# Streaming layer 3's factors in more and smaller pieces, and making layer 2's and 3's helper rows later

## Chip, cores and metric

The kernel runs on one core of a Trainium2 chip. The metric is the device time of one execution in microseconds (us); lower is better. The time of the kernel before is 2317.83 us, the median of three runs.

## What is computed

Four graph layers on 128 graphs of 64 nodes with 512 features, in float32. `x` is [128, 64, 512] and `adj` [128, 64, 64]. Every layer takes `h = relu(layernorm(x))` and adds its result to `x`. Cut to what matters:

```python
# layer 0: hypergraph convolution 512 -> 1024, relu, layernorm, convolution 1024 -> 512
H = (adj != 0); m = Be * (H^T (h @ W1)); ...
# layer 1: attention from a sum of two scores
s = (h @ w) @ a;  A = exp(leaky(8 * tanh((s_i + s_j) / 8))) * adj, normalised;  out = A @ h @ w
# layer 2: attention from queries and keys
weight = adj * exp((h Wq^T + bq) (h Wk^T + bk)^T), normalised;  out = weight @ (h Wv^T + bv)
# layer 3: diffusion over K = 3 steps
e = leaky_relu(sj + si + ab);  transition = A * exp(e), normalised      # sj, si = (h @ Wv + bv) @ aw halves
H = sum_k Xk @ Wk[k] + bk[k],  Xk = transition^k @ h;  out = relu(H)
```

## The kernel before

**Tiles and stages.** The 8192 rows (nodes) are worked in 16 groups (`NG`) of 512 rows, four tiles of 128 rows each. The first half of the kernel runs layers 0 and 1 for all groups and stores the result in DRAM (`xmid`); the second half loads it again and runs layers 2 and 3 for all groups. Large products use a scheme of seven block products in place of eight (`strassen` for layers 0 and 1, the matmul at line 691; `chained` for layer 2, line 930; `product` for layer 3, line 1124). A float32 matmul shows as two passes in the trace.

**Layer 3's products.** For each group, `layer3` forms seven products with the weights `Wk3`. Their weight side, the factors, doesn't fit on chip for all seven. During the first half `setup_w3` makes them once and stores them in DRAM: `fac[f][n]`, with 4 blocks in `n = 0` and 3 blocks in `n = 1` (`BLOCKS`), each block 3 x 128 x 128. In the second half, `product` streams them back for every group: one load for `n = 0` (768 KB), one for `n = 1` (576 KB), at line 1116, into a buffer `wf` of up to four blocks; three such places exist. A block is then three matmuls (six passes). In the last group (`g == NG - 1`) two more buffers, `sh` and `hT`, which no later layer needs, take a part of the pieces. So a group has 14 such loads, the kernel 224.

**The helper rows.** `setup_bq` makes the vector `gb_c` from `Wk` and `bq` (layer 2): four loads of 256 KB, four multiply-adds on VectorE (lines 492 and 494), a small matmul. `setup_l3` makes the two rows `c3_b` and the constant `kap` (layer 3): twelve loads of 256 KB, ten dots on VectorE (`dot`, line 392), two spreads over the partitions (`spread`, lines 458 to 461). Both use four temporary places `tmp`, which layer 0's transposes use as well, and both are placed ahead of the loop over the groups, with priorities near group 0's.

**What sets the order.** The code doesn't emit instructions at once. Each operation goes into a `Graph` with its engine, an estimated cost, its reads and writes, and a priority: `G.prio` (period of the group, advanced by `step` as the layer proceeds) plus a shift by the name of the part (`part(name)` looks it up in `AT`). `Graph.run` then simulates five engines, `PE`, `DVE`, `ACT`, `POOL` and `SP`, and at each step takes the operation that can start first, the lowest priority first among those that can start at the same time. It also assigns the buffer places. Its result is a fixed order of instructions on every engine; on the chip each engine runs its own in that order and waits on semaphores. All DMAs go through SP's queue. Where the plan sees TensorE idle for over 1 us, `fill` puts matmuls of ones (line 1199) there.

```python
def dma(kb, fn, r, w, issue=0.34, lat=2.0):
    return G.op("SP", max(kb / 380.0, issue), fn, r, w, lat)
```

Lines named in what follows: 338 loads into `tmp`; 355 loads of `x`; 592 and 594 the graph products of layers 0 and 1; 601 to 603 a transpose by DMA (a copy, the DMA at line 602, a copy); 995 a second load of `x` in layer 2; 1067 layer 3's product with the transition; 1091 and 1104 to 1106 VectorE's block differences; 1133 the copy out of PSUM; 1163 the stores of the result.

Of the kernel before, what the change touches and what calls it, by code (L numbers as in the profile page):

```python
# [14 lines left out]
P = 128  # L15
C = 64
D = 512
DH = 1024
T = 4
KD = D // P  # L20
# [151 lines left out]
def tile_adj_preln_d4(  # L172
# [6 lines left out]
    nc = tc.nc  # L179
    NG = adj.shape[0]  # L180
    G = Graph()
# [22 lines left out]
        ([("row", [P, D], 4)], [("sh", [P, 4, 2, 2 * P], 1)]),  # L204
        ([("wa", [P, D], 1)], [("q", [P, D], 1)]),
        ([("wp", [P, 4, P], 2)], [("bv", [P, D], 1), ("bk", [P, D], 1)]),
        ([("w2m", [P, 7168], 1), ("wm", [P, 3584], 1)], [("a3", [P, 3, KD, P], 4), ("wf", [P, 4, 3, P], 3)]),
    ]
    slots, after = {}, {}
    for tag, (shape, n) in SLOTS.items():  # L210
# [8 lines left out]
    for two in TWO:  # L219
        both = work.tile([P, max(sum(size(shape) * n for _, shape, n in tags) for tags in two)], F32,  # L220
                         name="_".join(tag for tags in two for tag, _, _ in tags))
        for tags in two:
            at = 0
# [31 lines left out]
    def c_mm(n, count):  # L255
        return 2 * count * max(n * 2 / 2400 + 0.0025, 0.111)
# [6 lines left out]
    def pe(cost, fn, r, w):  # L263
        return G.op("PE", cost, fn, r, w)
# [16 lines left out]
    def dma(kb, fn, r, w, issue=0.34, lat=2.0):  # L281
        return G.op("SP", max(kb / 380.0, issue), fn, r, w, lat)

    def quad(b):
# [2 lines left out]
    FILL, LAT = 0.5, 2.3  # L287


    STRETCH, PERIOD1, PERIOD2 = (2.4057, 23.1237, 14.6194, 5.0478), 88.385, 152.83  # L290
    AT = {
        "x0": -4649.81, "apart": 515.41, "w1": 891.32, "b1": 147.15, "w2": 1055.04, "w": 146.66, "c1": 74.0, "l0":
        181.27, "c2": 131.25, "l1": 1241.14, "c": -4314.2, "g0": -2118.58, "g1": -4213.04, "g2": -574.45, "g3":
        -1827.82, "g": -443.79, "bq": -420.39, "l3": -143.58, "wg": 627.97, "wp": 228.79, "beg0": -1054.79, "beg1":
        -138.73, "end00": 1.09, "end01": -86.62, "end11": 256.44, "new2": -124.9, "new3": 81.75, "end2": -68.63,
        "end3": -133.99, "load1": -63.98, "load2": 661.26, "m": -63.44, "h0": 2.91, "p0": 25.16, "z0": -386.05,
        "q0": 47.65, "y0": -4107.25, "h1": -19.07, "p1": 5.7, "z1": -84.16, "q1": 20.96, "y1": -130.14, "s": -234.6,
        "t0": -462.0, "e0": -467.09, "t1": -348.17, "e1": -282.93, "hT": 524.3, "sh": 245.53, "lq": 730.58, "pt":
        -113.04, "v": 589.88, "pv": 1100.8, "s3": 672.72, "tt": 1008.78, "a0": 690.15, "b0": 538.95, "a1": 811.73,
        "ws": 2002.18, "load3": 441.07, "bk": 299.55,  # L300
    }

    def part(name):
        G.shift = AT[name]
# [28 lines left out]
        dma(8, lambda: nc.sync.dma_start(sb, src), [], [name])  # L333
        return sb

    def load_tmp(tag, n, shape_of, src):
        b = Buf(tag)
        dma(n * P * 4 / 1024, lambda: nc.sync.dma_start(shape_of(b.t), src), [], [b])
        return b

    def temp(src):

        return load_tmp("tmp", D, lambda t: t, src)

    xt, adjs, xmid, rows = {}, {}, {}, []

# [43 lines left out]
    def dot(in0, in1, acc, r, w):  # L390
        j = Buf("o")
        dvp(0.77, lambda: nc.vector.scalar_tensor_tensor(j.t, in0(), 1.0, in1(), op0=ALU.mult, op1=ALU.mult,
                                                         accum_out=acc()), r, [*w, j])
# [89 lines left out]
            act(0.6, lambda c=c, e=e: nc.scalar.copy(e.t, ps[c].t), [ps[c]], [e])  # L483
            dma(256, lambda c=c, e=e: nc.sync.dma_start(wg_d[c * P:(c + 1) * P, :], e.t), [e], ["wg_d"])

    def setup_bq():

        pg, bk = Buf("ps"), Buf("o")
        for o in range(KD):
            k_ = temp(Wk[o * P:(o + 1) * P, :])  # L490
            if o == 0:
                dvp(0.45, lambda k_=k_: nc.vector.tensor_scalar(bk.t, k_.t, bq_c[:, 0:1], None, op0=ALU.mult), [k_, "bq_c"], [bk])
            else:
                dvp(0.85, lambda o=o, k_=k_: nc.vector.scalar_tensor_tensor(bk.t, k_.t, bq_c[:, o:o + 1], bk.t, op0=ALU.mult, op1=ALU.add),
                    [k_, "bq_c", bk], [bk])

        def mg():
            for c in range(KD):
                nc.tensor.matmul(pg.t[:, c:c + 1], bk.t[:, c * P:(c + 1) * P], ones[:, 0:1], start=True, stop=True)
        pe(c_mm(1, KD), mg, [bk], [pg])  # L500
        dve(0.2, lambda: nc.vector.tensor_copy(gb_c, pg.t[:, :KD]), [pg], ["gb"])

    def setup_l3():
        kk = Buf("mv")
        ab_t = load_tmp("rs", 1, lambda t: t, ab.partition_broadcast(P))
        for s in range(2):
            av, cc = temp(aw[s * D:(s + 1) * D].partition_broadcast(P)), Buf("col")
            bv_t = temp(bv3.partition_broadcast(P))
            dot(lambda bv_t=bv_t: bv_t.t, lambda av=av: av.t, lambda s=s: kk.t[:, s:s + 1], [bv_t, av], [(kk, s)])
            for c in range(KD):  # L510
                wv = temp(Wv3[c * P:(c + 1) * P, :])
                dot(lambda wv=wv: wv.t, lambda av=av: av.t, lambda c=c, cc=cc: cc.t[:, c:c + 1], [wv, av], [(cc, c)])
            spread(lambda cc=cc: cc.t, lambda s=s: c3_b[:, s, :], [(cc, c) for c in range(KD)], ("c3", s))
        dve(0.15, lambda: nc.vector.tensor_add(kap, kk.t[:, 0:1], kk.t[:, 1:2]), [(kk, 0), (kk, 1)], ["kap"])
        dve(0.15, lambda: nc.vector.tensor_add(kap, kap, ab_t.t), ["kap", ab_t], ["kap"])

# [492 lines left out]
    def layer3(g):  # L1009
# [66 lines left out]


        part("b0")
        sx = Buf("sx")
        keys = lambda i, v: [(a3[2 * i + v], n) for n in range(3)]  # L1080
        block = lambda i, j: [(lambda v=v: a3[2 * i + v].t[:, :, 2 * j:2 * j + 2, :]) for v in range(2)]
# [14 lines left out]
        def product(f, F, chain, first):  # L1096
            (A, B), (ka, kb) = F
            if first:
                banks[chain] = [Buf("ps"), Buf("ps")]
            X = Buf("xi")  # L1100
            lo, hi = (lambda f_: f_()[:, :, 0, :]), (lambda f_: f_()[:, :, 1, :])
            x2, x3, x4 = ((lambda i=i: X.t[:, i]) for i in range(3))
            sub = nc.vector.tensor_sub
            dvp(0.6, lambda: sub(x2(), lo(B), lo(A)), [*ka, *kb], [(X, 0)])
            dvp(0.6, lambda: sub(x3(), hi(B), x2()), [*kb, (X, 0)], [(X, 1)])
            dvp(0.6, lambda: sub(x4(), hi(A), x2()), [*ka, (X, 0)], [(X, 2)])
            lhs = {1: (lambda: lo(A), ka), 2: (lambda: hi(A), ka), 6: (x2, [(X, 0)]), 5: (lambda: lo(B), kb),
                   7: (x3, [(X, 1)]), 3: (x4, [(X, 2)]), 4: (lambda: hi(B), kb)}
            for n in range(2):
                w_, p, q = Buf(("wf", "sh", "wf", "hT", "wf")[(2 * f + n) % 5] if g == NG - 1 else "wf"), banks[chain][n], len(BLOCKS[n])  # L1110
                wv = lambda w_=w_, q=q: w_.t[:, :q] if w_.tag == "wf" else (
                    w_.t.rearrange("p a b c -> p (a b c)") if len(w_.t.shape) == 4 else w_.t.rearrange("p a b -> p (a b)"))[:, :q * 3 * P].rearrange(
                        "p (r k c) -> p r k c", r=q, k=3)
                shift = G.shift
                part("ws")
                dma(1000 if q == 4 else 850, lambda n=n, wv=wv: nc.sync.dma_start(
                    wv(), fac[f - 1][n].rearrange("p (r k c) -> p r k c", k=3, c=P)), [("fac", f - 1, n, k, d) for k in range(3) for d in FACS[n]] + ([(tt, 1)] if g == NG - 1 else []), [w_], lat=LAT)
                G.shift = shift
                for r, b in enumerate(BLOCKS[n]):
                    at, kl = lhs[b]  # L1120

                    def mm(at=at, r=r, p=p, wv=wv, q=q):
                        for k in range(3):
                            nc.tensor.matmul(inner(p, q)[:, r, :], at()[:, k, :], wv()[:, r, k, :], start=first and r == 0 and k == 0,  # L1124
                                             stop=k == 2, skip_group_check=True)
                    pe(c_mm(P, 3), mm, [*kl, w_] if first and r == 0 else [*kl, w_, p], [p])
                    step(c_mm(P, 3))

        def snapshot(chain):
            Z = Buf("zz")  # L1130
# [60 lines left out]
    def step(us):  # L1191

        G.prio += us * stretch[0]
# [19 lines left out]
    setup_l1()  # L1213
    part("c")
    W = combine(wm, w_sb, w_x, 2, D // 2, "DVE")
    part("bq")
    setup_bq()
    part("l3")
    setup_l3()
    for g in range(NG):  # L1220
        G.prio = g * PERIOD1
        if g:
            part("load1")
            load_group(g, x_in)
        for i, layer in ((0, layer0), (1, layer1)):
            stretch[0] = STRETCH[i]
            if g == 0:
                G.prio += AT["beg0" if i == 0 else "beg1"]
            if i == 0 and g == NG - 1:
                G.prio += AT["end00"]  # L1230
            if i == 1 and g >= NG - 2:
                G.prio += AT["end01" if g == NG - 2 else "end11"]
            layer(g)
        G.prio = g * PERIOD1
        part("wp")
        if g:
            for k in range(2):
                if 2 * g - 2 + k < 21:
                    setup_w3(2 * g - 2 + k, [("z", g - 1 + k, 1 - k)], [("z", g, k)])
# [83 lines left out]
```

## Time and profile before

| | |
|---|---|
| runs (us) | 2317.83, 2319.93, 2316.39 |
| profiled execution (us) | 2321.51 |
| its span, first to last instruction (us) | 2319.7 |
| mean granted TensorE clock | 0.999 |
| busy: PE, DVE, ACT, POOL (us) | 2279.9, 1865.1, 1393.2, 1190.9 |
| DMA | 355.12 MB, mean 153 GB/s |

PE is TensorE's matmuls and PEld its weight loads, DVE VectorE, ACT ScalarE, POOL GpSimd, SP the engine whose queue issues the DMAs. A group of instructions is told as line, engine, tiles written `<-` tiles read. `fac` is the factors in DRAM; the tiles of `wf` appear as `w2m_wm_a_wf`, since several tags share one piece of memory; for the same reason the tiles of `tmp` appear as `tmp_mB_xi`, those of `hT` as `z_hT` and those of `sh` as `row_sh`. A DMA issue line gives the count, the size of each and the median time from issue to landing. The chain of waits is the work that ended last, followed back from the last instruction. In a table by stretches, each row gives start:end, length, then the busy time of PE, PEld, DVE, ACT and POOL with the number of instructions in brackets, the granted clock, the busy share of the DMA engines and GB/s.

### The profile page before, as it was taken

To read this page: it belongs to the slowest core of one execution; us is meant where nothing else is said; L and a number is where in the kernel's file an instruction comes from. 1 tells how busy PE (TensorE), PEld (TensorE's weight loads), DVE (VectorE), ACT (ScalarE), POOL (GpSimd) and SP (SyncE) were. 2 spreads that over 40 slices of the span, in tenths; PEclk is the share of its full clock that TensorE was granted. 3 is DMA by queue.
4 is the path that set the end of the run, shared out by engine and by line. 5 is a ranking of instruction groups with operands and counts; after the bars stand their busy time and mean duration, and the time that the engine had idled before them with its cause. 6 is when DMAs were issued, how large, how long until landed. Compare 5 with 4: busy or idle time off the path is not lost.

```text
span 2319.7 us, 39752 instructions
## 1 busy us (share of the span) xinstructions
PE 2279.9 (98%) x14238; PEld 1866.4 (80%) x14238; DVE 1865.1 (80%) x4004; ACT 1393.2 (60%) x1993; POOL 1190.9 (51%) x1771
## 2 busy tenths in 40 slices
PE   8999999999999999999999999999999999999998
PEld 4676677776777767777688999999999989999898
DVE  7887877887778877787867888888888878788787
ACT  4766565675655765656657566566656655656542
POOL 7445556545665465543433455545455544545443
PEclk9999999999999999999999999999999999999999
DMA  6443233443333342323436877787787877878767
GB/s 232 103 104 77 78 98 79 102 90 79 83 91 94 90 90 58 74 71 68 97 98 161 223 222 229 234 223 213 226 244 213 235 215 217 222 224 225 200 200 242
DMA packets 403478, 355.12 MB, mean 153 GB/s; under 512 B 290896, under 2 KB 321872, under 8 KB 403280
## 3 DMA queue, kind: packets, MB, share of 16 engines
q1 hardware_dynamic: 403280, 352.58, 55.5%
q8 instruction: 112, 1.84, 0.3%
q14 instruction: 86, 0.70, 0.1%
HBM read 241.05 MB, written 44.33 MB: 123 GB/s over the span
## 4 chain that ended last, share of the span: by engine, by line
PE 84%; DMA 6%; DVE 5%; ACT 3%; issue 1%; POOL 1%; SPq 0%; DVEq 0%; ACTq 0%; POOLq 0%
PE ps L691 38%; PE ps L1124 19%; PE ps L930 15%; PE ps L592 4%; PE ps L844 2%; PE ps L1067 2%; DMA w2m_wm_a_wf<-fac 1%; DMA h<-o 1%; PE ps L999 1%; PE ps L961 1%; DMA x<-xm 1%; DMA z_hT<-tmp_mB_xi 1%; ACT h L583 1%; DVE st L562 1%; DMA tmp_mB_xi<-in_Wk_dram 0%
## 5 line engine op out<-in xcount | busy, mean ns | idle before, releaser
L583 ACT ACTIVATE h<-x,nm,rs 128x512 f32<-128x512 f32 x384 | 306.2, 812 | 234.9 <-POOL nm L570 220.3
L564 POOL TENSOR_SCALAR rs<-mv 128x1 f32<-128x1 f32 x320 | 104.6, 327 | 388.4 <-DVE mv L563 371.1
L1124 PE MATMUL ps<-w2m_wm_a_wf 128*128 128x128 f32 x2256 | 295.5, 277 | 3.8 <-DMA w2m_wm_a_wf<-fac 2.2
L1124 PEld LDWEIGHTS ps<-w2m_wm_a_wf 128*128 128x128 f32 x2256 | 275.8, 192 | 11.1 <-issue 4.0
L691 PE MATMUL ps<-w2m_wm_a_wf,s_s_zz 128*128 128x256 f32 x1152 | 274.8, 380 | 1.8 <-DVE s_s_zz L683 1.8
L1124 PE MATMUL ps<-w2m_wm_a_wf,tmp_mB_xi 128*128 128x128 f32 x1968 | 260.4, 277 | 9.8 <-DMA w2m_wm_a_wf<-fac 5.2
L1124 PEld LDWEIGHTS ps<-w2m_wm_a_wf,tmp_mB_xi 128*128 128x128 f32 x1968 | 243.2, 193 | 16.6 <-ACT h L583 7.5
L691 PEld LDWEIGHTS ps<-w2m_wm_a_wf,s_s_zz 128*128 128x128 f32 x1152 | 217.7, 190 | 39.7 <-issue 9.6
L691 PE MATMUL ps<-w2m_wm_a_wf,rT_vu_tt 128*128 128x256 f32 x1024 | 237.5, 380 | 2.0 <-ACT row_sh L453 0.7
L691 PE MATMUL ps<-wa_mem,mT_sx 128*128 128x512 f32 x512 | 238.1, 593 | 1.3 <-DMA wa_mem<-in_W1T_dram 1.0
L691 PEld LDWEIGHTS ps<-w2m_wm_a_wf,rT_vu_tt 128*128 128x128 f32 x1024 | 193.6, 190 | 48.5 <-issue 18.4
L565 POOL TENSOR_TENSOR rs<-rs,mhalf 128x1 f32<-128x1 f32 x320 | 209.2, 654 | 26.5
L562 DVE BATCH_NORM_STATS2 st<-x 128x6 f32<-128x512 f32 x256 | 176.1, 688 | 33.0 <-DMA x<-xm 25.7
L570 POOL TENSOR_SCALAR nm<-mv,rs 128x1 f32<-128x1 f32 x320 | 171.4, 537 | 30.2
L691 PE MATMUL ps<-wa_mem,s_s_zz 128*128 128x512 f32 x384 | 180.3, 593 | 0.0
L691 PEld LDWEIGHTS ps<-wa_mem,mT_sx 128*128 128x128 f32 x512 | 96.0, 191 | 103.9 <-issue 97.9
L818 ACT ACTIVATE z_hT<-z_hT 128x512 f32<-128x512 f32 x128 | 79.3, 630 | 133.6 <-DVE z_hT L711 133.6
L603 ACT COPY rT_vu_tt<-z_hT 128x1024 uint16<-128x1024 uint16 x128 | 146.7, 1162 | 16.6 <-DMA z_hT<-tmp_mB_xi 16.5
L719 POOL TENSOR_TENSOR u<-u,row_sh 128x256 f32<-128x256 f32 x96 | 75.4, 794 | 157.3 <-DVE u L661 134.7
L592 PEld LDWEIGHTS ps<-bd,h 128*128 128x128 f32 x1024 | 126.6, 192 | 36.4 <-issue 27.6
L885 POOL TENSOR_TENSOR x<-x,u 128x256 f32<-128x256 f32 x96 | 88.8, 950 | 113.0 <-DVE u L663 113.0
L601 ACT COPY o<-h 128x1024 uint16<-128x1024 uint16 x128 | 133.8, 1047 | 9.3 <-DVE h L1056 6.9
(205 smaller groups left out, 4991.8 us busy)
## 6 DMA issues: line engine op xcount, KB each, us to landing
w2m_wm_a_wf<-fac SPq DMA_DIRECT2D x110, 768.0 KB, 5.0
w2m_wm_a_wf<-fac SPq DMA_DIRECT2D x109, 576.0 KB, 4.8
x<-xm SPq DMA_DIRECT2D x128, 256.0 KB, 3.5
x<-in_x_dram SPq DMA_DIRECT2D x64, 256.0 KB, 2.8
xm<-x SPq DMA_DIRECT2D x64, 256.0 KB, 2.0
out_dram<-x SPq DMA_DIRECT2D x64, 256.0 KB, 3.9
adj<-in_adj_dram SPq DMA_DIRECT2D x32, 256.0 KB, 4.6
fac<-wp_bv_bk SPq DMA_DIRECT2D x63, 128.0 KB, 2.0
```

What stands on the lines that cost most here:

```text
L562: dve(0.69, lambda i=i: nc.vector.bn_stats(st.t[:, i, :], src(i)), [r[i]], [(st, i)])
L564: small(0.28, lambda: nc.gpsimd.tensor_scalar_add(rs.t, mv.t[:, 1:2], EPS), [mv], [rs])
L565: small(0.62, lambda: nc.gpsimd.tensor_tensor(rs.t, rs.t, mhalf, ALU.pow), [rs], [rs])
L570: small(0.32, lambda: nc.gpsimd.tensor_scalar(nm.t, mv.t[:, 0:1], rs.t, -1.0, op0=ALU.mult, op1=ALU.mult), [mv, rs], [nm])
L583: act(0.82, lambda: nc.scalar.activation(h.t, xx.t, AF.Relu, bias=nm.t, scale=rs.t), [xx, nm, rs], [h])
L592: nc.tensor.matmul(quad(p)[:, c, :], h.t[:, c * P:(c + 1) * P], rhs(), start=True, stop=True)
L601: act(1.05, lambda: nc.scalar.copy(u16(planes.t).rearrange("p (q c) -> p q c", q=2), u16(src()).rearrange("p (c q) -> p q c", q=2)), ksrc, ...
L603: act(1.16, lambda: nc.scalar.copy(u16(dst()).rearrange("p c (k q) -> p c k q", q=2), u16(back()).rearrange("p (q c r) -> p c r q", q=2, c ...
L691: nc.tensor.matmul(p.t[:, :n], lhs()[:, c, :], rhs(c), start=first and c == 0, stop=c == kc - 1, skip_group_check=True)
L885: pool(0.78, lambda: nc.gpsimd.tensor_add(xx.t[:, cols], xx.t[:, cols], U.t[:, iu]), [xx, u], [xx])
L930: nc.tensor.matmul(pair(p.t)[:, o, :], a, b, start=first and o == 0 and c == 0, stop=c == 1, skip_group_check=True)
L1124: nc.tensor.matmul(inner(p, q)[:, r, :], at()[:, k, :], wv()[:, r, k, :], start=first and r == 0 and k == 0, stop=k == 2, skip_group_check ...
```

## The change

- The streamed factors have pieces of two blocks (384 KB) or one (192 KB). A product has four loads: 2 and 2 blocks of `n = 0`, 2 and 1 of `n = 1`. `wf` has six places of two blocks, in the same memory as three of four blocks. In the last group, every eighth piece goes to `sh` and every eighth to `hT`. The plan's cost of a load goes from 1000 and 850 to 495 and 290.
- `setup_bq` is called after group 2's layers are put into the graph, and `setup_l3` in two halves after those of groups 3 and 4. Their loads wait (`when`) for an operation of layer 0 of that group (the last small operation before line 831's normalisation).
- Layer 3 of the last two groups gets a further shift of priority from its part `b0` on (`late3`, `last3`).
- All values of `STRETCH`, `PERIOD1`, `PERIOD2` and `AT` are other ones.

```diff
-        ([...], [("a3", [P, 3, KD, P], 4), ("wf", [P, 4, 3, P], 3)]),
+        ([...], [("a3", [P, 3, KD, P], 4), ("wf", [P, 2, 3, P], 6)]),
...
-    STRETCH, PERIOD1, PERIOD2 = (2.4057, 23.1237, 14.6194, 5.0478), 88.385, 152.83
+    STRETCH, PERIOD1, PERIOD2 = (2.471, 24.4862, 13.5943, 6.202), 83.899, 164.599
     AT = {
-        "x0": -4649.81, "apart": 515.41, "w1": 891.32, ...
+        "x0": -62.74, "apart": -18.5, "w1": -4.8, ...
...
-    def setup_bq():
+    def setup_bq(when):
...
-            k_ = temp(Wk[o * P:(o + 1) * P, :])
+            k_ = temp(Wk[o * P:(o + 1) * P, :], when)
...
-    def setup_l3():
-        kk = Buf("mv")
-        ab_t = load_tmp("rs", 1, lambda t: t, ab.partition_broadcast(P))
-        for s in range(2):
...
+    def setup_l3(s, when):
+        if not s:
+            sums.append((Buf("mv"), load_tmp("rs", 1, lambda t: t, ab.partition_broadcast(P), when)))
+        kk, ab_t = sums[0]
+        av, cc = temp(aw[s * D:(s + 1) * D].partition_broadcast(P), when), Buf("col")
+        bv_t = temp(bv3.partition_broadcast(P), when)
...
         part("b0")
+        if g >= NG - 2:
+            G.prio += AT["late3" if g == NG - 2 else "last3"]
...
-                w_, p, q = Buf(("wf", "sh", "wf", "hT", "wf")[(2 * f + n) % 5] if g == NG - 1 else "wf"), banks[chain][n], len(BLOCKS[n])
...
-                dma(1000 if q == 4 else 850, lambda n=n, wv=wv: nc.sync.dma_start(
-                    wv(), fac[f - 1][n].rearrange("p (r k c) -> p r k c", k=3, c=P)), ..., [w_], lat=LAT)
...
-                for r, b in enumerate(BLOCKS[n]):
...
+                p, q = banks[chain][n], len(BLOCKS[n])
+                for lead in range(0, q, 2):
+                    m, at_ = min(2, q - lead), 4 * f + 2 * n + lead // 2
+                    w_ = Buf({2: "sh", 6: "hT"}.get(at_ % 8, "wf") if g == NG - 1 else "wf")
...
+                    dma(495 if m == 2 else 290, lambda n=n, wv=wv, lead=lead, m=m: nc.sync.dma_start(
+                        wv(), fac[f - 1][n][:, lead * 3 * P:(lead + m) * 3 * P].rearrange("p (r k c) -> p r k c", k=3, c=P)),
+                        ..., [w_], lat=LAT)
...
+                    for r in range(lead, lead + m):
...
-    part("bq")
-    setup_bq()
-    part("l3")
-    setup_l3()
+    sums = []
     for g in range(NG):
...
         part("wp")
+        if g in (2, 3, 4):
+            part("bq" if g == 2 else "l3")
+            when = [("z", g, 0)]
+            setup_bq(when) if g == 2 else setup_l3(g - 3, when)
+            part("wp")
```

## The prediction

> **What bounds the kernel now.** I read the page first: busy shares, then the chain, then the DMA issues.
>
> ```profile
> span 2319.7 us, 39752 instructions
> ...
> PE 2279.9 (98%) x14238; PEld 1866.4 (80%) x14238; DVE 1865.1 (80%) x4004; ACT 1393.2 (60%) x1993; POOL 1190.9 (51%) x1771
> ...
> w2m_wm_a_wf<-fac SPq DMA_DIRECT2D x110, 768.0 KB, 5.0
> w2m_wm_a_wf<-fac SPq DMA_DIRECT2D x109, 576.0 KB, 4.8
> x<-xm SPq DMA_DIRECT2D x128, 256.0 KB, 3.5
> ```
>
> TensorE is busy 98% of the span, and the change takes no matmul away. So all it can win is TensorE's idle time, 2319.7 - 2279.9 = 39.8 us, and the 138 filler passes (line 1199) that the plan puts into gaps it foresees, about 0.112 us each, 15 us. A part of this cannot be had: the first loads and the last output (about 7 us after the last matmul).
>
> Where that time lies is seen in stretches of 58 us (PE busy is the second figure, DVE the fourth):
>
> ```profile
> 0.00:58.00 58.00, 51.11 (x204) 28.57 (x205) 41.58 (x88) 26.19 (x42) 41.10 (x59) 1.00 0.67 232
> 58.00:116.00 58.00, 55.17 (x209) 36.51 (x208) 51.67 (x103) 41.91 (x58) 25.11 (x35) 1.00 0.43 103
> 116.00:174.00 58.00, 56.29 (x275) 43.89 (x274) 48.56 (x114) 36.64 (x50) 26.93 (x44) 1.00 0.42 104
> 406.00:464.00 58.00, 58.00 (x258) 42.53 (x257) 47.30 (x108) 36.12 (x51) 29.68 (x48) 1.00 0.41 101
> 1218.00:1276.00 58.00, 54.52 (x415) 48.57 (x415) 44.55 (x106) 42.68 (x61) 21.39 (x42) 1.00 0.64 162
> 1856.00:1914.00 58.00, 54.78 (x486) 50.51 (x486) 46.07 (x100) 33.65 (x49) 27.41 (x38) 1.00 0.79 215
> 2204.00:2262.00 58.00, 55.82 (x523) 52.60 (x522) 50.55 (x108) 28.33 (x43) 24.64 (x32) 1.00 0.67 202
> 2262.00:2320.00 58.00, 48.51 (x458) 46.46 (x456) 42.35 (x78) 14.67 (x24) 21.89 (x27) 0.98 0.75 240
> ```
>
> The first half in its steady run (406 to 464) has no idle TensorE at all. The losses are the start, the turn from layer 1 to layer 2 (1218 to 1276), single bad groups of the second half (1856 to 1914) and the end. The granted clock is 1.00 nearly throughout, so the clock explains nothing.
>
> What TensorE waits for comes from its waits at line 1124, layer 3's products (us, times), and then from the chain between 1840 and 1925 us (start, length, what):
>
> ```profile
>   DMA w2m_wm_a_wf<-fac: 9.8, 11
> ```
>
> ```profile
> 1848.29 5.18 PE ps L930 x24
> ...
> 1884.84 4.88 DMA w2m_wm_a_wf<-fac
> ...
> 1892.97 4.89 PE ps L1124 x42
> ...
> 1903.38 6.13 DMA w2m_wm_a_wf<-fac
> ...
> 1919.66 5.18 PE ps L930 x24
> ```
>
> The block "L930 x24" comes once a group; in the chain of waits it starts at 1372.24, 1439.70 and so on to 2125.14 us. Eleven groups take 752.9 us, 68.4 each, and the quickest takes 67.46. So the steady second half loses 11 x 0.99 = 10.9 us. The group above takes 71.37, 3.9 too many, and two late factor loads stand in it. Two more long groups (69.46 and 68.33) hold such loads too; the three lose 6.8 us between them.
>
> **The pieces.** A piece is now 4 or 3 blocks in one of three places. Forty-two passes, one product of 7 blocks, take 4.69 us when nothing holds them. When a piece is used up, its place is refilled while TensorE works through the two other pieces, 7 blocks, 4.69 us. The refill takes 5.0 or 4.8 us from issue to landing. It is late by some tenths whenever no other work of TensorE comes between; that agrees with few, short waits: 11, 9.8 us. After the change there are six places of 2 blocks (one piece in four has 1). Five other pieces hold 8.75 blocks on average, 8.75 / 7 x 4.69 = 5.9 us. No row shows a load of 384 KB; it lies between 3.5 us (256 KB) and 4.8 us (576 KB), by their line 4.0. I take 4.0, and the margin goes from -0.3 to +1.9 us. Most of these waits should go. I take -6.5 us of the 9.8, about what the three long groups lose; the rest comes back as the next late thing, the transposes "h<-o", which stand in the chain of other groups. Bounds: 0 and -9.8.
>
> **A rule against it.** Landing grows only from 4.8 to 5.0 us for a third more bytes, so most of it is latency and sharing, which four pieces pay four times. The Trainium skill, page "DMA: Bandwidth & Descriptors", section Bandwidth, says to batch DMAs to at least 1 MiB, and its section on the anatomy gives about 2.0 us plus bytes / 436e3 for one DMA (there for GpSimd's path): by estimate 2.9 us for 384 KB, and four pieces of a product one after the other 11.1 us against 7.2 now, over 400 us more in 112 products. By the rows the loads aren't one after the other: 110 x 5.0 + 109 x 4.8 = 1073 us of landing alone, plus 128 x 3.5 for x, lie in a second half of some 1090 us, so several are in flight. I go by the rows.
>
> **More issues on SP.** 224 loads become 448. A load at line 1116 holds SP for 0.353 us (median): 224 x 0.353 = 79 us more over 1,090 us. Per group now: 14 x 0.353 + 8 transposes x 1.25 + some 16 loads, stores and rows at 0.4, about 21 of 68 us; after, 26. Cover: SP's free two thirds. Cost 0; without cover see the first rival. On TensorE a further wait on data that has landed shows no gap: the 42 passes of a product with two pieces go at 0.112 us each. Cost 0, upper bound 224 x 0.05 us, the PE semaphore row (51 ns), 11 us, if none overlapped.
>
> **The rows moved (setup_bq, setup_l3).** They ran between 51 and 105 us, where VectorE is at its fullest of the first half (51.67 of 58). There, VectorE does 4 multiply-adds (0.49 + 3 x 0.745), 10 dots (0.687 + 0.081) and 2 spreads at 0.68: 11.8 us, and SP 15 loads of 256 KB. TensorE idles 2.83 us in that stretch and 1.71 in the next, and runs 12 fillers at 97.93 (1.3 us) and 32 near 140 (3.6 us). One case is plain: the fillers at 97.93 and 1.2 us idle after them end with a VectorE subtraction that stood behind five dots and a spread (4.5 us). I take -4 us; bounds 0 and -9.4, everything just listed.
>
> In groups 2 to 4 the same 11.8 us meet 3 x 71.7 = 215 us, of which VectorE is free 19% (47.3 of 58 busy), 41 us. SP gets 15 x 0.43 us. The temporaries use the four "tmp" places that the transposes use too, and the offset op of the group gates the loads. Queued behind on VectorE are additions out of PSUM that TensorE's next product needs. Cover: VectorE's free 41 us. I take +1; bounds 0 and +11.8, all of it exposed.
>
> **Order, turn and end.** Every priority has another value, so each engine's order is new. The turn holds 3.5 us idle plus 36 fillers (4.0); the end, 2.2 + 9.5 - 7 idle plus 26 fillers (2.9), 7.6. Two new shifts act on layer 3 of the last two groups, so something moves there. I take -2; bounds -15.1 (all of both) and +6, two groups as bad as the one at 1856.
>
> **Sum.** -6.5 + 0 - 4 + 1 - 2 = -11.5 us. The profiled execution took 2321.51 us (span 2319.7 and 1.8 around it): 2310.0 after. The median, 2317.83, lies 3.7 lower: **2306.3 us**.
>
> **Rivals.** *SP's queue becomes the bound (slower).* SP works in order, and for 210.8 us a factor load at its head waits for TensorE to free a place ("SPq L1116 <- PE ps L1124", 134 times). Behind it stand transposes that TensorE's next layer 2 needs. If four of a group's 14 further issues stand before such a transpose and show on TensorE, 16 x 4 x 0.353 = 22.6 us: 2317.8 - 11.5 + 22.6 = 2328.9. For it: 51.1 us of ACT waits on "h<-o" already. Against: SP is free two thirds of the time, and TensorE waited for that step only 2.8 us in all. It decides as soon as over two issues per group show. Chance 0.22.
>
> *Another wait takes the factors' place (no change).* The group period stays at 68.4 since the transposes are late next; the start gives 3 us, the middle groups take 1: about 2316. Chance 0.15.
>
> *The edges close as well (much faster).* Recoverable: steady 10.9, start 9.4, turn 7.5, end 7.6, and 2.3 idle in the first 58 us after the first loads' 4.6, together 37.7; three quarters of it, 28: 2290. For it: fillers mark gaps that the plan itself knew of. Against: the turn's waits are for transposes and VectorE, which the change leaves. Chance 0.15.
>
> **How the numbers follow.** The forecast has 0.48, its own range 2297 to 2314. The range for 8 in 10 reaches over both outer cases, 2286 to 2331. About 0.2%, 4.6 us, is what a measurement can tell from no change here. Faster: 0.45 of the forecast and 0.15 of the edges, 0.60. Same: 0.16. Slower: 0.22 and what the middle groups or a worse order may add, 0.24.
>
> **What would show it.** Right: 448 loads at line 1116's successor, those of 384 KB landing near 4.0 us, TensorE's waits for "fac" under 4 us; groups of the second half near 67.6; PE busy in 58 to 116 above 56.5; first-half groups still 71.7. Wrong: "fac" waits of 10 us or more, ACT's waits on "h<-o" well above 51 us, TensorE idle in groups 2 to 4, or losses at the turn or the end above 8 us each. It would fall altogether if 384 KB took as long as 768.

## The result and the profile after

The kernel after takes 2308.96 us (median of six runs, 2307.24 to 2311.3) against 2319.41 for the kernel before: ratio 0.9957, 95% interval 0.9946 to 0.9969. That is 10.5 us less; 11.5 were forecast. The profiled execution took 2308.66 us, its span is 12.8 us shorter. Levels differ by some us between chips, so every experiment below is read by its ratio to the kernel before, which ran beside it on the same chip.

The page of the kernel after, the lines that answer to those of before:

```profile
span 2306.9 us, 40150 instructions
...
PE 2277.5 (99%) x14234; PEld 1862.5 (81%) x14234; DVE 1884.4 (82%) x4004; ACT 1388.4 (60%) x1993; POOL 1195.1 (52%) x1771
...
w2m_wm_a_wf<-fac SPq DMA_DIRECT2D x329, 384.0 KB, 4.1
...
w2m_wm_a_wf<-fac SPq DMA_DIRECT2D x112, 192.0 KB, 3.8
```

TensorE's idle time went from 39.8 to 29.4 us, which is 10.4 of the 12.8 us; the products are the same, with four fillers fewer. The pieces land in 4.1 and 3.8 us. What TensorE waited for at layer 3's products (line 1132 now; us, times):

```profile
  DVE tmp_mB_xi L1108: 7.4, 12
...
  DMA w2m_wm_a_wf<-fac: 1.8, 5
```

Waits for factors fell from 9.8 to 1.8 us (3.5 in a second trace of this kernel, `after_again`), but VectorE's block differences are late there now. The stretches (PE busy is the second figure, DVE the fourth):

```profile
0.00:58.00 58.00, 51.58 (x184) 27.30 (x185) 43.75 (x86) 31.46 (x47) 41.52 (x56) 1.00 0.65 221
58.00:116.00 58.00, 56.63 (x241) 39.17 (x240) 50.10 (x101) 45.99 (x63) 31.73 (x46) 1.00 0.30 69
116.00:174.00 58.00, 58.00 (x270) 43.34 (x269) 46.06 (x103) 31.75 (x47) 36.71 (x52) 1.00 0.33 90
290.00:348.00 58.00, 55.20 (x235) 38.60 (x234) 47.34 (x104) 32.52 (x46) 31.80 (x45) 1.00 0.46 109
1856.00:1914.00 58.00, 58.00 (x504) 54.07 (x503) 49.34 (x101) 36.17 (x55) 30.21 (x45) 1.00 0.78 221
```

The start is fuller, the bad group near 1856 is gone, and there is a new hole at 290 to 348, where `setup_l3` now runs.

To see where the 12.8 us lie I took two milestones of every group from the timelines: the end of layer 0's last product (line 844 before, 846 after) and the end of layer 3's product with the transition (1067 and 1069).

| milestone | before (us) | after (us) | after - before |
|---|---|---|---|
| layer 0, group 0 | 121.6 | 109.7 | -12.0 |
| layer 0, group 3 | 336.2 | 326.4 | -9.8 |
| layer 0, group 4 | 407.9 | 401.8 | -6.1 |
| layer 0, group 13 | 1054.0 | 1048.4 | -5.6 |
| layer 3, group 1 | 1333.9 | 1333.7 | -0.2 |
| layer 3, group 12 | 2087.5 | 2081.9 | -5.7 |
| last matmul | 2312.8 | 2300.6 | -12.2 |
| span | 2319.7 | 2306.9 | -12.8 |

So: the start wins 9.8, the middle groups give back 3.7, the turn from layer 1 to layer 2 gives back 5.4, the steady second half wins 5.5, the end 6.5, and 0.6 lie after the last matmul.

Two cautions. Each of these figures comes from one trace. In `after_again` (span 2313.4 us) the differences to the kernel before at the same milestones are -8.3 (layer 0, group 3), -3.5, -2.6, +3.5, -0.5 and -5.7 (last matmul): 8.3 won at the start, 4.8 and 6.1 given back, 4.0 and 5.2 won. The signs repeat, the sizes only to one or two us. Against another trace of the old second half they can be less: in `before_rows_left_out`, where it is unchanged, the end (layer 3 of group 12 to the last matmul) takes 220.3 us, 225.2 in the kernel before, 218.7 and 220.1 in the kernel after. So the end's 6.5 us are the least sure. And a milestone tells when one product ended, not how much other work TensorE had done by then. That is seen in its idle time and its fillers up to the same milestones:

| from the start to the end of layer 0 of | before: idle us, fillers | after: idle us, fillers |
|---|---|---|
| group 0 | 9.7, 30 | 7.8, 40 |
| group 3 | 12.4, 70 | 8.8, 40 |
| group 4 | 12.4, 70 | 10.7, 46 |

At 0.112 us a filler, the 12.0 us at group 0 hold a gain of only 0.8: the new order does other work of TensorE later. Of the 9.8 at group 3, 7.0 are idle time and fillers saved, of the 6.1 at group 4, 4.4.

### The profile page after: what moved, and what is told of

The parts are those of the page before. It is cut to its first block, busy times and chain, and to the rows that moved or that the text cites. A ratio compares the mean times of both kernels' runs of the same rounds, so it can differ in the third digit from the quotient of the medians.

```text
span 2306.9 us, 40150 instructions
## 1 busy us (share of the span) xinstructions
PE 2277.5 (99%) x14234; PEld 1862.5 (81%) x14234; DVE 1884.4 (82%) x4004; ACT 1388.4 (60%) x1993; POOL 1195.1 (52%) x1771
## 4 chain that ended last, share of the span: by engine, by line
PE 84%; DMA 5%; DVE 5%; ACT 2%; POOL 1%; issue 1%; SPq 0%; DVEq 0%; POOLq 0%; ACTq 0%
PE ps L693 38%; PE ps L1132 20%; PE ps L932 14%; PE ps L594 5%; PE ps L846 2%; PE ps L1001 2%; PE ps L1069 2%; DMA x<-xm 1%; DMA h<-o 1%; DMA rw<-row 1%; PE ps L963 1%; DMA out_dram<-x 1%; PE ps L477 1%; DVE rT_vu_tt L1038 1%; DVE st L564 1%
## 5 line engine op out<-in xcount | busy, mean ns | idle before, releaser
L1132 PE MATMUL ps<-w2m_wm_a_wf 128*128 128x128 f32 x2304 | 303.5, 276 | 1.2 <-DMA w2m_wm_a_wf<-fac 0.6
L1132 PEld LDWEIGHTS ps<-w2m_wm_a_wf 128*128 128x128 f32 x2304 | 282.3, 192 | 8.0 <-issue 1.2
L1132 PE MATMUL ps<-w2m_wm_a_wf,tmp_mB_xi 128*128 128x128 f32 x1932 | 256.0, 276 | 3.0 <-DVE tmp_mB_xi L1108 2.8
L693 PEld LDWEIGHTS ps<-w2m_wm_a_wf,s_s_zz 128*128 128x128 f32 x1152 | 217.3, 190 | 40.9 <-issue 10.2
L1132 PEld LDWEIGHTS ps<-w2m_wm_a_wf,tmp_mB_xi 128*128 128x128 f32 x1932 | 239.4, 192 | 10.1 <-DVE tmp_mB_xi L1108 4.6
L567 POOL TENSOR_TENSOR rs<-rs,mhalf 128x1 f32<-128x1 f32 x320 | 220.9, 690 | 26.2
L572 POOL TENSOR_SCALAR nm<-mv,rs 128x1 f32<-128x1 f32 x320 | 152.8, 478 | 31.1
L594 PEld LDWEIGHTS ps<-bd,h 128*128 128x128 f32 x1024 | 127.5, 192 | 33.3 <-issue 22.0
L603 ACT COPY o<-h 128x1024 uint16<-128x1024 uint16 x128 | 132.6, 1046 | 11.4 <-DVE h L1060 6.4
```

Of the source, the lines that this page charges most:

```text
L567: small(0.62, lambda: nc.gpsimd.tensor_tensor(rs.t, rs.t, mhalf, ALU.pow), [rs], [rs])
L572: small(0.32, lambda: nc.gpsimd.tensor_scalar(nm.t, mv.t[:, 0:1], rs.t, -1.0, op0=ALU.mult, op1=ALU.mult), [mv, rs], [nm])
L594: nc.tensor.matmul(quad(p)[:, c, :], h.t[:, c * P:(c + 1) * P], rhs(), start=True, stop=True)
L603: act(1.05, lambda: nc.scalar.copy(u16(planes.t).rearrange("p (q c) -> p q c", q=2), u16(src()).rearrange("p (c q) -> p q c", q=2)), ksrc, ...
L693: nc.tensor.matmul(p.t[:, :n], lhs()[:, c, :], rhs(c), start=first and c == 0, stop=c == kc - 1, skip_group_check=True)
```

## The experiments

In all of them "ratio" is the time against that of the kernel before on the same chip, with its 95% interval; the quotient of the two medians lies up to 0.0007 from it. Where an experiment keeps the order, the plan is the same and only what an operation issues differs; where a priority or a size in the plan differs, the whole order is planned anew.

| kernel | median us | kernel before beside it, us | ratio | 95% |
|---|---|---|---|---|
| kernel after | 2308.96 | 2319.41 | 0.9957 | 0.9946 to 0.9969 |
| before_factors_kept | 2309.60 | 2323.19 | 0.9936 | 0.9923 to 0.9949 |
| after_factors_kept | 2302.93 | 2323.19 | 0.9909 | 0.9894 to 0.9924 |
| before_half_loads | 2308.19 | 2323.19 | 0.9931 | 0.9917 to 0.9944 |
| after_twice_issues | 2307.33 | 2323.19 | 0.9929 | 0.9915 to 0.9943 |
| after_again | 2312.99 | 2325.04 | 0.9951 | 0.9937 to 0.9966 |
| before_rows_left_out | 2320.43 | 2325.04 | 0.9987 | 0.9975 to 0.9998 |
| after_rows_left_out | 2313.39 | 2325.04 | 0.9952 | 0.9938 to 0.9965 |
| after_no_late | 2323.72 | 2325.04 | 1.0000 | 0.9990 to 1.0009 |
| before_half_again | 2309.94 | 2324.62 | 0.9933 | 0.9919 to 0.9946 |
| before_block_loads | 2309.37 | 2324.62 | 0.9930 | 0.9916 to 0.9944 |
| new_start_half_loads | 2319.14 | 2324.62 | 0.9980 | 0.9967 to 0.9992 |
| w1_early_half_loads | 2314.28 | 2323.09 | 0.9964 | 0.9952 to 0.9976 |

### What are the factor loads worth?

**before_factors_kept**

```diff
-    dma(..., lambda n=n, wv=wv: nc.sync.dma_start(
+    dma(..., lambda n=n, wv=wv: None if g else nc.sync.dma_start(
```

> The kernel before, every instruction in the same order, but the factor loads of groups 1 to 15 are left out: the products of those groups multiply what lies in the places. Theory A (the late factor loads cost what the three long groups lose): TensorE's waits for fac go from 9.8 us to about 0, the median falls by 6 to 11 us, to 2308 to 2313. Theory B (another wait takes their place, so the loads are not what the time hangs on): 2316 to 2320. Theory C (SP's queue and the shared DMA engines are also what makes transposes and x late): more than 12 us, below 2307.

Ratio 0.9936: about 15 us, more than theories A and B gave. TensorE's waits for factors are gone. By the ratio the loads cost the kernel before more than the 9.8 us of waits that carry their name; TensorE's idle time in the trace fell by 10.5 us, from 39.8 to 29.3. The interval, 12 to 18 us, lies above A's range and reaches into C's.

**after_factors_kept**, the same edit in the kernel after.

> The kernel after, same order, with the factor loads of groups 1 to 15 left out in the same way. Theory A: the pieces have already taken this loss away, so little is left: 0 to 3 us below the kernel after, 2306 to 2309. Theory B: 0. Theory C (the 448 issues and their traffic cost time elsewhere, so that the change gave away a part of its gain): 5 us or more below, 2304 or less.

Ratio 0.9909 against 0.9957 and 0.9951 for the kernel after: 10 to 11 us less still. By the ratios theory A's "0 to 3" is wrong and C's "5 or more" holds: with few waits of TensorE for factors left, the loads still cost time. How much is less sure. Beside the one variant of the kernel after that ran on the same chip (after_twice_issues, 2307.33 us) it is 4.4 us, and TensorE's idle time in the traces fell by 2.7 us, from 29.4 to 26.7. Who waited for other DMAs shows where. First the waits of the kernel after, then those without its factor loads (us, times, longest):

```profile
ACT w2m_wm_a_wf L605 <- DMA wa_q<-o: 38.7, 32, 3.1
DVE st L564 <- DMA x<-xm: 31.8, 35, 2.7
DVE ee L763 <- DMA rw<-row: 28.6, 16, 2.5
ACT z_hT L605 <- DMA h<-o: 28.4, 28, 3.1
```

```profile
ACT w2m_wm_a_wf L605 <- DMA wa_q<-o: 20.2, 19, 2.5
...
DVE st L564 <- DMA x<-xm: 20.1, 19, 3.3
...
ACT z_hT L605 <- DMA h<-o: 7.5, 6, 3.1
DVE ee L763 <- DMA rw<-row: 7.2, 9, 1.7
```

127.5 us of such waits become 55.0. Most of them are hidden behind TensorE's work, some are not. The edit takes two things away, and no run parts them. One is the traffic on the DMA engines: the transposes "h<-o" land in 3.2 us in place of 4.2, the loads of x in 3.0 in place of 3.6. The other is SP's standing at a factor load until its place is free ("SPq L1123 <- PE ps L1132"), 308.7 us in the kernel after and 12.5 without the loads. That it is not all landing shows at "rw<-row": it lands scarcely sooner (median of the 28 issued after 1270 us, 3.1 us with the loads and 2.9 without), yet its waits fell from 28.6 to 7.2 us, so it was issued sooner for its reader; either of the two can do that.

### Piece size or places?

**before_half_loads**

```diff
+        def halves(to, src, q):
+            for s in (slice(0, 2), slice(2, q)):
+                nc.sync.dma_start(to[:, s], src[:, s])
...
-                dma(1000 if q == 4 else 850, lambda n=n, wv=wv: nc.sync.dma_start(
...
+                dma(1000 if q == 4 else 850, lambda n=n, wv=wv, q=q: halves(wv(), ...
```

> The kernel before, its order, its three places and its priorities, but each factor load is issued as two, one after the other: 2 and 2 blocks, 2 and 1 blocks, 384 or 192 KB each, so that the first blocks wait for the first half alone. Places still come free whole. Theory A (size: the first half lands near 4.0 us in place of 5.0 and that is what TensorE waits for): fac waits fall from 9.8 to below 4 us, median 4 to 7 us lower, 2312 to 2315. Theory A' (places: the gain of the change comes from places coming free in smaller steps, and halves alone don't help): within 2 us of the kernel before. Rival SP: 224 further issues of 0.35 us stand before transposes, 5 to 20 us slower.

Ratio 0.9931: this edit alone, with the old places, the old order and the rows still at the start, wins 15 us by the ratio, more than the 10.5 of the whole change, and as much as leaving the loads out. Its page and its DMA issues:

```profile
span 2305.5 us, 40303 instructions
...
PE 2275.9 (99%) x14238; PEld 1863.0 (81%) x14238; DVE 1870.1 (81%) x4004; ACT 1394.8 (60%) x1993; POOL 1189.9 (52%) x1771
```

```profile
w2m_wm_a_wf<-fac SPq DMA_DIRECT2D x329, 384.0 KB, 4.4
w2m_wm_a_wf<-fac SPq DMA_DIRECT2D x109, 192.0 KB, 3.7
```

In the trace, the first half lands 4.1 us after its issue (median of 224), where the whole piece took 4.9; the second half lands 5.1 us after the first one's issue. So splitting brings the first blocks 0.8 us sooner and the last ones hardly later. By the milestones its first half is that of the kernel before (layer 0 of group 15: +1.8 us), layer 3 goes from +0.6 in group 0 to -9.0 in group 13, and the end wins 4.9 more. TensorE's waits for factors are 1.2 us (3.0 in the repetition), and its idle time falls by 10.2 us, from 39.8 to 29.6. The other 4 us of the shorter span are not idle time: the same matmuls were busy for 2275.9 us in place of 2279.9, in a trace taken on another occasion (2277.9 in the repetition). So theory A is confirmed, and its size was too small; that 15 us come from the loads is shown by the ratio, but the traces show only 10 of them as idle time. A' (places) is refuted as the cause in this order; SP's further issues do no harm. **before_half_again** repeated it with 0.9933:

> The kernel before with each factor load issued as two halves, as in before_half_loads, again, on the chip of the two that follow. All theories: ratio to the kernel before 0.992 to 0.994.

**before_block_loads**: `for s in [slice(r, r + 1) for r in range(q)]`, seven loads a product.

> The kernel before, its order and places, with each factor load issued block by block: 4 and 3 loads of 192 KB, 784 in all. Theory A (TensorE's waits were for landing, and halves have taken all of them): the same as halves within 2 us. Theory S (the shorter the first load, the more is gained, also where halves already land in time): another 3 us or more. Rival SP (560 issues more than before, a whole product's seven in a row ahead of transposes): 5 us or more slower than halves.

Ratio 0.9930: nothing more than halves give, and nothing lost with 784 loads. Theory A. The loads land in 3.8 us (median), scarcely sooner than 384 KB:

```profile
w2m_wm_a_wf<-fac SPq DMA_DIRECT2D x767, 192.0 KB, 3.8
```

**after_twice_issues**

```diff
+        def halves(to, src, m):
+            for s in ((slice(0, 1), slice(1, 2)) if m == 2 else (slice(0, 1),)):
+                nc.sync.dma_start(to[:, s], src[:, s])
...
```

> The kernel after, its order, but every load of two blocks is issued as two loads of one block (192 KB): 784 loads in place of 448. It doubles the cost in dispute of the slower rival. Theory A (SP has free time, issues are hidden): 0 to +3 us on the kernel after, 2309 to 2312. Rival SP (issues ahead of transposes show on TensorE at 1.4 us per 4 issues a group): 336 / 224 x 22.6 = about 34 us more, 2343.

Ratio 0.9929: not slower; if anything it is 5 us quicker than the kernel after (0.9957 and 0.9951, measured on other occasions; its interval stays clear of the first's by 0.0003 and overlaps the second's, so this gain is not shown). The slower rival of the prediction is refuted: a further 336 issues cost nothing that can be seen, where it asked for 34 us.

### The rows

**before_rows_left_out**

```diff
+        o.eng, o.cost, o.fn, o.prio = eng, cost, (lambda: None) if self.mute else fn, self.prio + self.shift
...
+    G.mute = True
     part("bq")
     setup_bq()
     part("l3")
     setup_l3()
+    G.mute = False
```

With `G.mute` an operation is planned, but issues nothing.

> The kernel before, its order, with setup_bq and setup_l3 planned but not issued; the vector, the rows and the constant are set to 0.01. It takes the rows out of the start without any other order. Theory A (crowding: the start is quicker since VectorE and SP lose this work): layer 0 of group 1 ends 4 us or more earlier, and the median is 3 to 6 us lower. Theory P (order: the 10 us that the start has won come from the other priorities of the loads and of the first products): under 1.5 us.

Ratio 0.9987, about 3 us (0.5 to 6; the medians are 4.6 apart), and in the trace layer 0 of group 1 ends only 1.0 us earlier. The median is within theory A's 3 to 6, the milestone is not within its 4 or more. In the trace the 3 us are not at the start. VectorE did get lighter, and TensorE did not get busier (54.40 against 55.17 before, with the spreads' own passes gone):

```profile
58.00:116.00 58.00, 54.40 (x201) 35.62 (x200) 42.07 (x77) 42.45 (x58) 24.49 (x37) 1.00 0.30 53
```

The case that the prediction called plain is there too. The hole after the 12 fillers, in the kernel before and then without the rows:

```profile
100.65 2.00 PE L691 MATMUL ps<-w2m_wm_a_wf,s_s_zz 128*128 128x256 f32 x8 [1.22 <-DVE s_s_zz L683]
```

```profile
99.40 1.99 PE L695 MATMUL ps<-w2m_wm_a_wf,s_s_zz 128*128 128x256 f32 x8 [1.69 <-DVE s_s_zz L687]
```

With the dots and the spread away TensorE still waits for the same subtraction, 1.7 us. So in this order VectorE's load by the rows isn't what made TensorE idle at the start; by the traces that is theory P. The run can't tell about the fillers: they belong to the plan, which still counts the rows, and all 70 of them up to group 3 stay.

**after_rows_left_out**, the same in groups 2 to 4; **after_again** is its control.

> The kernel after, its order, with setup_bq and setup_l3 planned but not issued, and the same constants. Theory A (the rows' 11.8 us of VectorE delay what TensorE needs in groups 3 and 4: the waits of 0.9 us at 301 and 1.9 us at 341 us): the 3.7 us that layer 0 lost between group 3 and group 4 come back, fillers apart, so 2 to 4 us below the kernel after. Theory P (these waits belong to the new order): under 1 us.

> The kernel after, unchanged, so that its variants stand beside it on the same chip. All theories: 2304 to 2311, the ratio to the kernel before between 0.994 and 0.997.

The control's ratio is 0.9951. From the end of layer 0 of group 2 to that of group 4 the kernel after takes 149.2 us, its repetition 151.3, and without the rows 146.7; two steady groups take 143.4. So the rows cost 2.5 to 4.7 us there, as theory A says, 1.7 of it the two spreads' passes on TensorE. But theory A's 2 to 4 us on the whole time are not there (0.9952 and 0.9951): what these groups win is given back later. The timeline of the kernel after shows the place (start, length, what, idle before it):

```profile
300.96 1.99 PE L693 MATMUL ps<-w2m_wm_a_wf,rT_vu_tt 128*128 128x256 f32 x8 [0.91 <-ACT u L661]
...
341.03 1.99 PE L693 MATMUL ps<-w2m_wm_a_wf,rT_vu_tt 128*128 128x256 f32 x8 [1.89 <-ACT u L661]
```

### The start

No run that keeps the order wins the start's 9.8 us, so they come with the new order. TensorE's first product of layer 0, and the load of its weights on SP; the kernel before (TensorE's timeline, then SP's):

```profile
30.69 3.67 PE L691 MATMUL ps<-wa_mem,mT_sx 128*128 128x512 f32 x8 [0.98 <-DMA wa_mem<-in_W1T_dram]
```

```profile
20.90 1.00 SPq L321 DMA_DIRECT2D wa_mem<-in_W1T_dram  x2
```

and the kernel after:

```profile
19.28 1.93 PE L693 MATMUL ps<-wa_mem,mT_sx 128*128 128x512 f32 x4
```

```profile
5.53 1.05 SPq L321 DMA_DIRECT2D wa_mem<-in_W1T_dram  x2
```

Layer 0's weights are asked for 15.4 us sooner and its first product begins 11.4 us sooner. By the table of idle time and fillers this is mostly other work put later: up to group 0 only 0.8 us are saved, and 6.2 of the 7.0 lie between group 0 and group 3, where the kernel before has 2.7 us idle and 40 fillers and the kernel after 1.0 and none. Two kernels tried to tell what of the order does it.

**new_start_half_loads**: old pieces and places with halves, rows in groups 2 to 4, priorities of the start nearer to those of the kernel after (`"x0": -872.5, "w1": -74.53, "c": 137.83, "g0": -2318.66, "g1": -5586.89`), those of the second half in part as before (`v`, `s3`, `b0`, `lq`) and in part far from both (`ws`, the factor loads, 3904.37 for 2002.18 before and 2114.56 after; `load3` -3066.07 for 441.07 and 1391.55).

> A try at a better version: the old pieces and places, each load issued as two halves, the rows made in groups 2 to 4, and the order of the start, the loads and the first products led by priorities near those of the kernel after; the second half's priorities near those of before. Theory P (the start's 10 us come from that order, and are independent of what the halves win): layer 0 of group 0 ends about 10 us earlier than in the kernel before, a part is lost in groups 2 to 4, and the median lies 3 to 8 us below halves alone, ratio to before 0.989 to 0.992. Theory N (what the start wins is given back at the turn, as in the kernel after): the same as halves within 2 us.

Ratio 0.9980. The start wins 13.8 us at layer 0 of group 0 (theory P's part), but 11 of them are gone by group 15, and the second half wins only 4 more where halves won 16. On the median it is some 9 to 11 us slower than halves alone, and its trace is of its quickest run; neither theory's number is met. TensorE still waits 5.3 us for factors here, where halves in the order of before left 1.2 and 3.0: the halves' gain is not independent of the order. As a better version it failed.

**w1_early_half_loads**

```diff
-        "x0": -4649.81, "apart": 515.41, "w1": 891.32, ...
+        "x0": -4649.81, "apart": -18.5, "w1": -4.8, ...
...
```

> The kernel before with halves of the factor loads, the rows still made early, and two priorities changed to those of the kernel after: w1 from 891.32 to -4.8 and apart from 515.41 to -18.5, so that the loads of layer 0's first weights come sooner in SP's queue; the rest of the order follows from that. Theory W (the start's 10 us come from the time at which W1T is loaded: 20.9 us in the kernel before, 5.5 us in the kernel after, and the first product of layer 0 at 30.7 and 19.3 us): W1T issued before 10 us, the first product before 24 us, group 0's layer 0 done 6 us or more earlier than in the kernel before. Theory R (it takes the rows' move, since they fill SP and VectorE there): group 0 less than 3 us earlier. On the median: up to 6 us below halves if it keeps the gain, as slow as 5 us above if the rest of the order gives it back.

Ratio 0.9964, some 7 us above halves. W1T is loaded at 6.8 us and the first product stands at 24.6 us, but group 0 ends at 121.9 us, no earlier than before, and group 1 is 6.2 us late. Here too the early product saves nothing: up to group 0 TensorE idles 12.6 us and runs 36 fillers. In its timeline the loads of `Wq` and `Wk` come after x, and TensorE stands for 5.1 us:

```profile
10.16 9.51 PE L477 MATMUL ps<-tmp_mB_xi 128*128 128x512 f32 x16 [5.10 <-DMA tmp_mB_xi<-in_Wk_dram]
```

Theory W is not enough: W1T early alone does not win the start. Theory R's number, less than 3 us, is what came, and R is not ruled out: no run moves the rows and keeps the other priorities of the start. Shown is that the work of the rows, taken out of the order of before, does not win it; whether the new priorities or the rows' absence from the plan do stays open.

### The end

**after_no_late**

```diff
-        "ws": 2114.56, ... "late3": 826.6, "last3": 1219.64,
+        "ws": 2114.56, ... "late3": 0.0, "last3": 0.0,
```

> The kernel after with late3 and last3 set to 0, so that layer 3 of the last two groups has no further shift; the order of the groups before is nearly the same. Theory L (the 6.9 us won at the end come from these shifts): 5 us or more slower than the kernel after, 2314 or more. Theory A (they come from the pieces, through fac waits of the last groups that went away): within 3 us of the kernel after.

Ratio 1.0000: without the two shifts the whole gain is gone, 11 us on the control. Until layer 3 of group 13 the trace is within 3 us of the kernel after; from there it loses 11.8. TensorE runs out of other work, as its timeline shows:

```profile
2257.59 4.85 PE L1207 MATMUL ps<-ones 128*128 128x128 f32 x42
2265.31 1.10 PE L753 MATMUL ps<-ee,ones 64*64 64x256 f32 x4 [2.87 <-DVE ee L748]
2266.33 5.69 PE L1207 MATMUL ps<-ones 128*128 128x128 f32 x34
```

Fillers and idle time stand before layer 3's transition product of the last group, which ends at 2278.9 us; in the kernel after it ends at 2262.3 us, and until then TensorE still has products of group 14 to do. Theory L, within this set of priorities; the shifts were not tried in the order of before. Nor does it say that they win the 6.5 us by which the end beats the kernel before: halves in the order of before, without any such shift, win 5.9 over the same stretch (from layer 3 of group 12 to the last matmul).

### The turn

The 5.4 us lost between layer 0 of group 13 and layer 3 of group 1 were not taken apart by a run. TensorE's own figures for that stretch, first of the kernel before, then of the kernel after:

```profile
1100.00:1340.00 240.00, 235.56 (x1531) 200.35 (x1530) 185.69 (x401) 147.19 (x213) 100.83 (x166) 1.00 0.55 142
```

```profile
1094.00:1340.00 246.00, 238.93 (x1548) 202.24 (x1548) 186.07 (x407) 148.65 (x215) 103.89 (x169) 1.00 0.54 142
```

Idle time is 7.1 us in place of 4.4, and the fillers, 52 in place of 42, add 1.1; together 3.7 of the 5.4. What waits first there stays open.

## Why the prediction was right, point by point

**Bound and total.** TensorE was the bound and stayed so; 10.4 of the span's 12.8 us came out of its idle time. The total, -11.5 us, was right to 1 us on the median. That is partly luck. One term was right in place (the pieces); the others were off in both directions and cancelled: by the milestones the start won 5.8 more than I took, and the middle and the turn gave back 2.7 and 5.4.

**The pieces: -6.5 us.** The mechanism holds: a refill of 5.0 us against 4.69 us of other work. Factor waits fell to 1.8 us (under 4 was asked), 384 KB landed in 4.1 us (4.0 was taken by the line between 256 and 576 KB), groups of the second half take 68.0 us on the mean of eleven (67.6 was asked, 68.5 before on the same milestones, so half of the way), and the steady second half won 5.5 us. That size is from the best of the traces: TensorE's idle time between layer 3 of group 1 and of group 12 is 7.5 us in the kernel before, 2.2 in the kernel after, but 4.0 in its repetition and 5.8 in after_rows_left_out, whose second half is the same; 2.0 and 1.6 with halves alone in the order of before, 0.9 without the loads. No run puts the old pieces into the new order, so that the pieces win this in the kernel after is argued from the same waits, and shown only in the order of before. There halves alone are worth 15 us by the ratio, outside the bound of 9.8; by TensorE's idle time it is 10.2, of which some 4 lie at the end, which I had put elsewhere. And places, of which my sum of 8.75 blocks spoke, were not needed for it: earlier landing of the first blocks was enough.

**The rule against it.** For 192 KB I gave no measured value; the issue lines say 3.8 us. The Trainium skill, page "DMA: Bandwidth & Descriptors", section on the anatomy of one DMA, would give 2.9 and 2.5 us for 384 and 192 KB, an estimate from its fit for GpSimd's path; here, on SP's queue with several transfers in flight, 4.1 and 3.8 us were measured. Its section Bandwidth asks for batches of 1 MiB or more, for 75% of the peak rate; here loads of 768 and 576 KB, the same as halves, and single blocks of 192 KB, in one order, gave ratios of 1, 0.9931 and 0.9930. In this kernel the number of loads did not matter, and the landing of the first did.

**More issues on SP: 0.** Right. 336 more again cost nothing; the slower rival, at 0.22, had no ground in its issues. I gave it that much since SP stood at the head of its queue for 210.8 us. That standing grew to 308.7 us and the kernel still got quicker; whether it is a part of what the loads still cost (after_factors_kept) stays open.

**The rows moved: -4 and +1.** The step failed in its reason. I read VectorE's fullest stretch as the cause of TensorE's gaps; the rows taken out of the start give 1 us there, and the hole that I called plain stays (1.7 us). The place and the bound were right: of the 9.4 us that I listed as idle time and fillers, 7.0 were saved up to group 3, with the new order. In the middle the rows cost 2.5 to 4.7 us, 3.7 by the milestones, above the 1 that I took and within its bound; TensorE idle in groups 2 to 4 was a sign that I had named, and it came (55.20 busy of 58 from 290 us, 57.41 before). VectorE's free time, 40 us (18% of 215, not 19%), was a mean, and a product of layer 0 waited twice for a copy out of PSUM. The rows have 16 loads of 256 KB, not 15; nothing rests on it.

**Order, turn and end: -2.** The sum of its parts is -1.1 (turn +5.4, end -6.5), so the value holds and its parts don't, which is luck. Without the two new shifts, which the text only named as something that moves, the end of this order loses 11 us; how the 6.5 divide between them, the pieces and the scatter of the traces stays open.

**The rivals.** "Another wait takes the factors' place" is partly true: waits for "wa_q<-o" rose from 21.2 to 38.7 us and for "rw<-row" from 9.1 to 28.6, "h<-o" fell from 51.1 to 28.4. That they cost a part of the gain is likely, and not shown. "The edges close as well" came true at the start and the end, not at the turn.

**A better version.** Halves on the kernel before (0.9931 and 0.9933) lie 0.2% below the change (0.9957 and 0.9951), on other occasions; the intervals touch those of the first figure and overlap those of the second. It is at least as quick. It is a few more lines and needs no new order.

## What to carry to other kernels

When a stream's refill is only just longer than the work that covers it, try first to split the load so that the first consumer waits for its own part, before touching buffers or order: here that alone won at least as much as the whole change. Don't take the waits that carry a load's name for a bound on what it costs: leaving the loads out of the kernel after still won 3 to 11 us, by the measure taken, where 1.8 us of such waits were left. Where an order is planned anew, read the milestones group by group, and beside them the idle time and the fillers up to each: an early milestone can be nothing but work done in another order (12.0 us at group 0, 0.8 of it saved), and gains at the start and losses at the turn of this size are easily taken for the effect of the edit that was meant.

## What was not expected of the hardware

A load of 192 KB landed hardly sooner than one of 384 KB (3.8 and 4.1 us), and those of 576 and 768 KB took 4.8 and 5.0: four times the bytes cost 1.2 us more here. Two halves issued one behind the other were complete 5.1 us after the first issue, against 4.9 for the whole. And with the factor loads away the transposes landed sooner, by an amount that goes with the order: "h<-o" in 3.2 us in place of 4.2 and "wa_q<-o" in 3.1 in place of 3.9 in the order of after, 3.2 in place of 3.4 and 3.2 in place of 3.7 in that of before.
